# A two-layer graph network on one core: bias by a TensorE product, the row factor folded into the edge weights, and a later sort of the early tiles

## The chip, the cores and the metric

The kernel runs on one core of a Trainium2 chip. The engines that matter here are TensorE (PE), VectorE (DVE), ScalarE (ACT), GpSimd (POOL) and SyncE (SP), which only issues DMAs. Each has its own queue of instructions and works through it in order; they meet at semaphores. The metric is the device time of one execution in microseconds (us), as a median over runs.

## The reference, cut to what matters

N is 4096 nodes, D is 512 features. Every row of `adj` has its diagonal and some eight other entries above zero, all below one.

```python
a = adj + eye(N)
d = sum(a, axis=1) ** (-0.5)
out = (d[:, None] * a * d[None, :]) @ x @ W.T + b     # layer 0
x = layernorm(x + relu(out))
# layer 1: scores masked by max(adj, eye) with 1e16, so that with entries
# below one each node attends to itself alone
x = layernorm(x + x @ wv @ wo)
```

With y = d · (x Wᵀ), row t of layer 0 is d_t · Σ_k w_k · y[col_k] + (d_t · a_tt + d_t) · y_t + b. The first sum goes over the entries off the diagonal.

## The kernel before, in words

Only `few_edges_below_one` runs in the profile; `general` stands behind a test of the data. The 4096 rows are 32 tiles of 128 rows. `adj` is dense in memory (2 MB a tile), and the kernel looks for the few entries itself.

**First pass** (the loop over t in range(NT + 1)). SP loads every tile of `adj` (L545). POOL loads x (L550), PE transposes it (L673) and multiplies it by Wᵀ (L687), ACT copies between (L678), scales the product by d and so makes y (L720), and POOL writes y to memory (L722). ACT also sums the rows of a tile (L694) or, for a tile that DVE scans in this pass, looks for negative entries (L699). `scaling` makes d on POOL (L706, L709).

DVE finds the entries. A tile's *scan* is 16 steps: for each of eight segments of 512 columns one MAX8 (L749) and one FIND_INDEX8 (L750). Its *sort* is some 25 small operations (L753 to L811) over 64 candidates a row. It leaves in `rec` the columns, the weights w and their splits into bf16 pieces. The operations of a sort stand between the steps of the next tile's scan, in the generator `steps`. Then a tile is *matched*: `match` runs six stages (KEY to END, L825 to L876) that permute the rows by their number of edges with small bf16 products on PE (L858, L861) and end in `cols_all` (L872), the columns to be gathered, KH = 9 slots a row.

`EARLY` = 12 tiles are scanned in the first pass as they come, then the five last ones, which stay resident, then the 15 of `again`, which are loaded a second time. `order` is that order, and place n means the n-th tile of it. `RATE` = 7 steps of `steps` are emitted per iteration of the first pass; the rest is spread over the tiles of the second.

**Second pass** (the loop over i in range(NT + 2)). For place i POOL issues nine indirect DMAs (L1077), each of which gathers 128 rows of y; they run up to 18 ahead of PE. ACT builds nine 128 × 128 matrices s_t from the weights (L973 to L986). PE adds up nine products g · s_t (L1280; two records each in the profile). DVE does L1139 (yo ← yo · own + b, with the bias in `b_bc`), L1146 (h ← acc · d + yo) and L1154 (h ← max(h, 0) + x, with its row sum). PE transposes h (L673), ACT copies it (L678), PE multiplies by the product of the two weights of layer 1 (L687), and ACT scales and writes out (L1185). L1173 and L1176 make the variance on DVE. For the last two places DVE sums gathered rows first (`presum`, L1096), and PE's products are at L1104.

SP's queue in the second pass holds, for each place, the load of `yo` (y of the tile itself; three buffers, so it waits for an L1146 three places back) and that of x (which waits for an L1154), and between them the reloads of `adj` (five buffers, which wait for DVE and ACT to be done with an older tile). A reload is issued in the code where `steps` comes to a tile that isn't there.

Of the kernel before, what the change touches and what calls it, by code (L numbers as in the profile page):

```python
# [9 lines left out]
FP = mybir.dt.float32  # L10
# [4 lines left out]
P = 128  # L15
# [404 lines left out]
def few_edges_below_one(  # L420
# [44 lines left out]
    small = ctx.enter_context(tc.tile_pool(name="small", bufs=4))  # L465
    big = ctx.enter_context(tc.tile_pool(name="big", bufs=5))
    wk_ = ctx.enter_context(tc.tile_pool(name="work0", bufs=1))
    recs = ctx.enter_context(tc.tile_pool(name="recs", bufs=8))
    keys = ctx.enter_context(tc.tile_pool(name="keys", bufs=2))
    dram = ctx.enter_context(tc.tile_pool(name="dram", bufs=1, space=bass.MemoryType.DRAM))  # L470
    mt = ctx.enter_context(tc.tile_pool(name="match", bufs=1))
# [78 lines left out]
        engine.dma_start(x_t, x[ts(t, P), :])  # L550
        return x_t

    EARLY, LAG = 12, 5
    last = NT - LAG
    early = [e * last // EARLY for e in range(EARLY)]

# [15 lines left out]
    w_nat, wv = su0[:, 0], su0[:, 1].rearrange("p c d -> p (c d)")  # L572
    nc.scalar.dma_start(w_nat, w0.rearrange("(c p) d -> p c d", p=P))
    wT = p1.tile([P, ND, D], FP, name="wT", bufs=1)
    b_bc = const.tile([P, D], FP, name="b_bc")
    wvo = const.tile([P, ND, D], FP, name="wvo")

    def transpose_w():
        for dc in range(ND):
            pt = ps_t.tile([P, 512], FP, name="pt")  # L580
            for oc in range(ND):
                nc.tensor.transpose(pt[:, ts(oc, P)], w_nat[:, oc, ts(dc, P)], ident)
            nc.scalar.copy(wT[:, dc, :], pt[:, :D])

    def load_second_weights():

# [138 lines left out]

        return rec.bitcast(BF)[:, :, 1::2]

    def extraction(t, a_t, rec):

        v = v_all[:, t, :]
        vu = v.bitcast(U32)
        idx = keys.tile([P, C], U32, name="idx")
        key = keys.tile([P, 2, C], U32, name="key")
        keyf = key.bitcast(FP)
        top = keys.tile([P, 2, K], FP, name="top")
        topu = top.bitcast(U32)
        own = keys.tile([P, E], FP, name="own")  # L740
        mask = keys.tile([P, C], FP, name="mask")
        ints = keys.tile([P, 2, K], U32, name="ints")
        w = rec[:, 1]
        home = slice(t // TS * E, (t // TS + 1) * E)
        long = []
        for s in range(SEGS):
            o = slice(s * E, (s + 1) * E)
            seg = a_t[:, ts(s, SW)]
            long.append(lambda o=o, seg=seg: nc.vector.max(v[:, o], seg))  # L749
            long.append(lambda o=o, seg=seg: nc.vector.max_index(idx[:, o], v[:, o], seg))  # L750

        def stt(out, a, sc, b, op0, op1, **kw):
            return lambda: nc.vector.scalar_tensor_tensor(out, a, sc, b, op0=op0, op1=op1, **kw)  # L753

        def both(a):
            return a.rearrange("p (o c) -> p o c", o=1).to_broadcast([P, 2, a.shape[1]])

        def one(out, a, s1, s2, **kw):
            return lambda: nc.vector.tensor_scalar(out, a, s1, s2, **kw)

        def top8(f, r):
            return lambda: nc.vector.max(top[:, f, r * 8 : r * 8 + 8], keyf[:, f])  # L762

        def drop(f, r):
            return lambda: nc.vector.match_replace(  # L765
                keyf[:, f], top[:, f, r * 8 : r * 8 + 8], keyf[:, f], 0.0
            )

        short = [
            [  # L770

                stt(own, idx[:, home], spot[:, t % TS : t % TS + 1], v[:, home],
                    ALU.is_equal, ALU.mult, accum_out=own_all[:, t : t + 1]),
                stt(key[:, 0], idx, 12, place[:, 0], ALU.logical_shift_left, ALU.bitwise_or),
            ],
            [
                stt(key[:, 1], vu, 0x7FFFF, place[:, 1], ALU.bitwise_and, ALU.bitwise_or),
                stt(key[:, 0], vu, 19, key[:, 0], ALU.logical_shift_right, ALU.bitwise_or),
            ],
            [stt(keyf, both(v), 0.0, keyf, ALU.is_gt, ALU.mult)],  # L780
            [stt(keyf[:, :, home], both(own), 0.0, keyf[:, :, home], ALU.is_equal, ALU.mult)],
            [
                top8(1, 0),
                lambda: nc.scalar.activation(
                    mask, keyf[:, 0], AF.Sign, accum_out=n_all[:, t : t + 1]
                ) if second else nc.vector.tensor_scalar(
                    mask, keyf[:, 0], 0.0, 0.0, op0=ALU.is_gt, op1=ALU.add,
                    accum_out=n_all[:, t : t + 1],
                ),
            ],  # L790
            [drop(1, 0), top8(0, 0)],
            [top8(1, 1), drop(0, 0)],
            [drop(1, 1), top8(0, 1)],
            [top8(1, 2), drop(0, 1)],
            [top8(0, 2)],
            [
                one(ints[:, 1], topu[:, 0], 0xFFF, 19, op0=ALU.bitwise_and,
                    op1=ALU.logical_shift_left),
                one(ints[:, 0], topu[:, 0], 12, 0xFFF, op0=ALU.logical_shift_right,
                    op1=ALU.bitwise_and),  # L800
            ],
            [
                stt(w.bitcast(U32), topu[:, 1], 0x7FFFF, ints[:, 1],
                    ALU.bitwise_and, ALU.bitwise_or),
                lambda: nc.vector.tensor_copy(rec[:, 0], ints[:, 0]),
            ],
            [one(rec[:, 2], w, 0.0, row1n, op0=ALU.is_gt, op1=ALU.mult)],
            [lambda: nc.vector.tensor_tensor(
                rec[:, 3:6], rec[:, 0:3], upper(rec)[:, 0:3], ALU.subtract
            )],  # L810
            [lambda: nc.vector.tensor_tensor(  # L811
                rec[:, 6], rec[:, 4], upper(rec)[:, 4], ALU.subtract
            )],
        ]
        return long, short


    second = []
# [99 lines left out]

    def steps():

        after = [[] for _ in range(STEPS)]
        for n, t in enumerate(order):
            if t not in a_tiles:
                reload()
            edges[t] = dict(rec=recs.tile([P, 7, K], FP, name="rec"))
            long, short = extraction(t, a_tiles[t], edges[t]["rec"])
            begun.append(t)
            for j in range(STEPS):
                long[j]()
                for f in after[j]:  # L930
                    f()
                if j == STEPS - 1:
                    picked.append(t)
                    if t in early:
                        nc.vector.tensor_reduce(
                            deg_all[:, t : t + 1], v_all[:, t, :], AX.X, ALU.add
                        )
                yield
            after = [[] for _ in range(STEPS)]
            for j, fs in enumerate(short):  # L940
                after[j] += fs
            after[len(short)].append(lambda t=t: sorted_.append(t))
        for fs in after:
            for f in fs:
                f()
            yield
# [41 lines left out]

    xs, us = {}, {}
    DEEP = 3  # L990
    RATE = 7
    EARLIER = NT - 7
    due = [(t + 1, t) for t in range(NT) if t not in early]
    for n, t in enumerate(early):
# [15 lines left out]
    for t in range(1, DEEP):  # L1010
        a_tiles[t] = load_first(t)
    transpose_w()
    nc.gpsimd.dma_start(b_bc, bcast_rows(b0, D))
    setup, left = iter(()), None
    for t in range(NT + 1):
        if t == 0:
# [12 lines left out]
            pts.append(transpose_rows(xs.pop(j)))  # L1029
        kind, begin, end = next(setup, (None,) * 3) if len(ahead) < 2 else (None,) * 3  # L1030
        got = begin() if kind == "t" else None
        for j in [j for at, j in due if at == t and j in early]:
            scaling(j)
        if t < NT:
            if t in early:
                sum_negative(t, a_tiles[t])
# [63 lines left out]
    def summed_products(i, pos, c=slice(0, D)):  # L1100

        k = SAME + pos if pos < KH - SAME else None
        g = slots[i * KH if k is None else i * KH + k]
        nc.tensor.matmul(  # L1104
            zs[i][:, c], mats[i][:, KH if k is None else k, :], g[:, c],
            start=(pos == 0), stop=(k is None),
        )

    def build(count):
# [24 lines left out]
        d = d_all[:, t : t + 1]  # L1134
        nc.scalar.activation(own, own, AF.Identity, scale=d, bias=d)  # L1135

    def own_bias(i):
        own = own_all[:, order[i] : order[i] + 1]
        nc.vector.scalar_tensor_tensor(yo[i], yo[i], own, b_bc, op0=ALU.mult, op1=ALU.add)  # L1139

    HALVES = (slice(0, D // 2), slice(D // 2, D))

    def scaled(i, c=slice(0, D)):
        if i not in hs:
            hs[i] = p2.tile([P, D], FP, name="h", bufs=3)
        nc.vector.scalar_tensor_tensor(  # L1146
            hs[i][:, c], zs[i][:, c], d_all[:, order[i] : order[i] + 1], yo[i][:, c],
            op0=ALU.mult, op1=ALU.add,
        )

# [95 lines left out]
    for i in range(NT + 2):  # L1246
        if i < NT:
            zs[i] = ps_a.tile([P, D], FP, name="acc")
        free = len([t for t in scanned if t in picked])
        p = i - 1  # L1250
        has_p = 0 <= p < NT
        for k in range(KH):
# [7 lines left out]
            if i == NT - 1:  # L1260
# [6 lines left out]
                if k == 7:  # L1267
                    pts[i] = transpose_rows(hs[i], (0, 1))
                if k == 8:
                    for n in range(KH - SAME + 1):  # L1270
                        summed_products(i, n, HALVES[1])
                    hTs[i] = p2.tile([P, ND, P], FP, name="hT", bufs=2)
# [6 lines left out]
            elif i < NT:  # L1279
                nc.tensor.matmul(  # L1280
                    zs[i], mats[i][:, k, :], slots.pop(i * KH + k),
                    start=(k == 0), stop=(k == KH - 1),
                )
            if i < NT:
                gather(i * KH + k + AHEAD)
# [26 lines left out]
            t = at("V", i, k)  # L1312
            if t is not None:
                variance(t)
            if k == 6 and i < NT:
                own_bias(i)
            if k == 6 and has_p:
                eps_var(p)
            t = at("F", i, k)
# [45 lines left out]
```

## Time and profile before

| what | value |
|---|---|
| time, median of 3 runs | 649.07 us (648.53 to 650.29) |
| profiled execution, its own time | 647.33 us |
| span of the profile | 645.5 us |
| PE busy | 556.8 us, 86% |
| DVE busy | 543.6 us, 84% |
| ACT busy | 509.1 us, 79% |
| POOL busy | 351.2 us, 54% |
| mean granted PE clock | 0.944 |
| DMA | 222.14 MB, mean 344 GB/s |

A line of the costliest groups names the code line, the engine, the operation, output and inputs and the number of instructions; after the bar stand busy time in us and mean duration in ns, and then the engine's idle time just ahead of them with what ended it. A line of a timeline has its start and duration in us, and in brackets the idle time ahead of it. DVE operations overlap by some 0.08 us, so from start to start they take less than their duration.

### The profile page before, as it was taken

The page shows a single profiled execution, that of the slowest core. Times are in us where ns is not written, and L with a number is a line of the kernel's source. Part 1 is how long each engine was busy: PE and PEld are TensorE (multiplying, and loading weights), DVE is VectorE, ACT ScalarE, POOL GpSimd, SP SyncE. Part 2 cuts the span into 40 slices and gives each one's busy share as a digit, 9 for nine tenths or more (in the row PEclk, how much of TensorE's full clock was granted, in tenths as well). Part 3 has the DMA queues.
Part 4 walks back from the last instruction along what each step waited for, and adds up shares of the span by engine and source line. Part 5 has one row for each costly group of instructions (what it writes and reads, how often), then busy time and mean ns, then how long its engine had stood idle before and what let it go on. Part 6 is the DMA issues. An engine that isn't in the chain of part 4 may idle for free. (4 is left out here: it accounts for less than half of the span.)

```text
span 645.5 us, 7946 instructions
## 1 busy us (share of the span) xinstructions
PE 556.8 (86%) x1604; PEld 258.0 (40%) x1604; DVE 543.6 (84%) x2141; ACT 509.1 (79%) x1121; POOL 351.2 (54%) x464
## 2 busy tenths in 40 slices
PE   1698696888689486999999989999999999999794
PEld 1344342444244132444443434444444444444352
DVE  5679999999999994999999979999999996532431
ACT  1868888779779775999898957999979989994433
POOL 5132421323232377767666757766767777777700
PEclk9599998799879886999999989999999999999798
DMA  8999999999999289999999898999999988888721
GB/s 332 391 427 422 428 421 426 424 421 422 422 428 395 102 263 366 340 411 408 399 401 405 324 391 302 380 382 360 365 404 341 340 268 272 292 270 253 243 70 54
DMA packets 51850, 222.14 MB, mean 344 GB/s; under 512 B 8080, under 2 KB 9104, under 8 KB 45520
## 3 DMA queue, kind: packets, MB, share of 16 engines
q1 hardware_dynamic: 18416, 119.55, 45.6%
q0 software_dynamic: 28240, 92.56, 40.8%
q10 hardware_dynamic: 5136, 9.44, 3.8%
q14 instruction: 43, 0.35, 0.2%
q8 instruction: 15, 0.25, 0.2%
HBM read 204.73 MB, written 16.78 MB: 343 GB/s over the span
## 5 line engine op out<-in xcount | busy, mean ns | idle before, releaser
L1077 POOL DMA_INDIRECT g<-y,cols_all x288 | 281.4, 977 | 112.6 <-issue 41.9
L1280 PE MATMUL acc<-g,s_t 128*128 128x512 f32 x540 | 258.1, 612 | 23.8 <-DMA g<-y,cols_all 13.4
L749 DVE MAX8 v_all<-a_t 128x8 f32<-128x512 f32 x256 | 172.7, 687 | 16.9 <-DMA a_t<-in_adj_dram 16.9
L750 DVE FIND_INDEX8 idx<-v_all,a_t 128x8 uint32<-128x512 f32 x256 | 175.9, 691 | 0.0
L1280 PEld LDWEIGHTS acc<-g,s_t 128*128 128x128 f32 x540 | 98.0, 194 | 140.9 <-issue 92.8
L687 PE MATMUL acc<-wT,xT 128*128 128x512 f32 x256 | 126.6, 647 | 24.1 <-ACT xT L678 24.0
L699 ACT ACTIVATE dump<-a_t 128x2048 uint8<-128x2048 f32 (+1 forms) x52 | 119.5, 2299 | 4.4 <-DMA a_t<-in_adj_dram 4.3
L687 PE MATMUL acc<-wvo,hT 128*128 128x512 f32 x256 | 118.6, 606 | 5.0 <-ACT hT L678 4.6
L687 PEld LDWEIGHTS acc<-wT,xT 128*128 128x128 f32 x256 | 51.1, 207 | 86.9 <-issue 58.1
L687 PEld LDWEIGHTS acc<-wvo,hT 128*128 128x128 f32 x256 | 49.7, 196 | 67.4 <-issue 58.1
L973 ACT ACTIVATE sq<-cols,wr_all 128x128 f32<-128x128 f32 x160 | 58.1, 396 | 0.3 <-ACT hT L678 0.2
L694 ACT ACTIVATE dump<-a_n 128x4096 uint8<-128x4096 f32 x15 | 54.4, 3628 | 4.7 <-DMA a_n<-in_adj_dram 4.6
L977 ACT ACTIVATE s_t<-sq,wr_all 128x128 f32<-128x128 f32 x128 | 57.6, 487 | 0.5
L550 POOL DMA_DIRECT2D x_t<-in_x_dram x32 | 18.0, 562 | 68.1 <-PE pt L673 67.5
L986 ACT ACTIVATE s_t<-s_t,wr_all 128x128 f32<-128x128 f32 x150 | 48.9, 394 | 0.0
L1146 DVE SCALAR_TENSOR_TENSOR h<-acc,d_all,yo 128x512 f32<-128x512 f32 (+1 forms) x33 | 24.0, 727 | 20.9 <-PE acc L1280 15.9
L762 DVE MAX8 top<-key 128x8 f32<-128x64 f32 x192 | 41.0, 221 | 0.5
L678 ACT COPY hT<-pt 128x512 f32<-128x512 f32 x31 | 17.9, 579 | 23.8 <-PE pt L673 22.8
L706 POOL TENSOR_SCALAR deg<-deg_all 128x1 f32<-128x1 f32 x32 | 6.8, 224 | 48.0 <-ACT dump L694 47.9
L1139 DVE SCALAR_TENSOR_TENSOR yo<-yo,own_all,b_bc 128x512 f32<-128x512 f32 x32 | 23.8, 743 | 7.7 <-ACT own_all L1135 7.7
L673 PE MATMUL pt<-ident,x_t 128*128 128x128 f32 x128 | 20.3, 291 | 8.8 <-DVE above L841 7.6
L765 DVE MATCH_REPLACE8 key<-top,key 128x64 f32<-128x64 f32 x128 | 27.2, 214 | 0.0
(128 smaller groups left out, 643.5 us busy)
## 6 DMA issues: line engine op xcount, KB each, us to landing
a_t<-in_adj_dram SPq DMA_DIRECT2D x30, 2048.0 KB, 17.2
a_n<-in_adj_dram SPq DMA_DIRECT2D x15, 2048.0 KB, 17.4
x_t<-in_x_dram POOLq DMA_DIRECT2D x32, 256.0 KB, 11.9
yo<-y SPq DMA_DIRECT2D x32, 256.0 KB, 5.3
x_t<-in_x_dram SPq DMA_DIRECT2D x32, 256.0 KB, 5.6
out_dram<-r_t ACTq DMA_DIRECT2D x32, 256.0 KB, 6.4
g<-y,cols_all POOLq DMA_INDIRECT x288, 7.3
y<-y_t POOLq DMA_DIRECT2D x17, 256.0 KB, 11.9
```

Of the source, the lines that this page charges most:

```text
L687: nc.tensor.matmul(u, srcT[:, dc, :], w[:, dc, :], start=(dc == 0), stop=(dc == ND - 1))
L694: nc.scalar.activation(dump[:, : part.shape[1]], part, AF.Copy, accum_out=dst)
L699: nc.scalar.activation(dump[:, o], a_t[:, o], AF.Relu, scale=-1.0, accum_out=neg_all[:, t, halves[0] : halves[0] + 1],)
L749: long.append(lambda o=o, seg=seg: nc.vector.max(v[:, o], seg))
L750: long.append(lambda o=o, seg=seg: nc.vector.max_index(idx[:, o], v[:, o], seg))
L762: return lambda: nc.vector.max(top[:, f, r * 8 : r * 8 + 8], keyf[:, f])
L765: return lambda: nc.vector.match_replace(keyf[:, f], top[:, f, r * 8 : r * 8 + 8], keyf[:, f], 0.0)
L973: nc.scalar.activation(sq, cols1, AF.Square, bias=wr[:, 2, k : k + 1])
L977: nc.scalar.activation(s_t[:, k, :], away(), AF.Relu, scale=wr[:, 3, k : k + 1], bias=wr[:, 1, k : k + 1],)
L986: nc.scalar.activation(s_t[:, k, :], s_t[:, KH, :], AF.Copy, scale=wr[:, 1, k : k + 1])
L1077: nc.gpsimd.indirect_dma_start(out=slots[j], out_offset=None, in_=y[:, :], in_offset=bass.IndirectOffsetOnAxis(ap=cols_all[:, t, k : k + 1 ...
L1280: nc.tensor.matmul(zs[i], mats[i][:, k, :], slots.pop(i * KH + k), start=(k == 0), stop=(k == KH - 1),)
```

## The change

- The bias leaves DVE. `split_b` writes b as three bf16 pieces into the three rows of `b3`, whose sum is b exactly, with five short DVE operations ahead of the first pass; the broadcast load of `b_bc` goes. In the second pass a product of `ones3` (3 × 128) with `b3` (3 × 512), both bf16, starts each accumulation on PE (`bias`), and the nine products are added to it. `own_bias` goes.
- The row factor d is multiplied into the weights w in the sort (a new DVE operation on 128 × 24), and L1146 becomes h ← yo · own + acc.
- `EARLY` goes from 12 to 14, so 13 tiles are reloaded and not 15; `RATE` goes from 7 to 9.
- `extraction` is divided into `scan` and `sorting`. `sort_some` decides how many waiting tiles are sorted during a scan: none for places 0 and 1, one each for places 2 to 6 (`FULL`), none for 7 to 17, two each from 18 (`HELD`) on. So five tiles are sorted before place 7, and the others in the second pass. The scans' index results wait in 15 `idx` buffers instead of 2; `recs` has 5 buffers instead of 8.
- `scaling` of an early tile is emitted right after the last step of its scan.

```diff
@@ -465,7 +465,7 @@
-    recs = ctx.enter_context(tc.tile_pool(name="recs", bufs=8))
+    recs = ctx.enter_context(tc.tile_pool(name="recs", bufs=5))
     keys = ctx.enter_context(tc.tile_pool(name="keys", bufs=2))
     dram = ctx.enter_context(tc.tile_pool(name="dram", bufs=1, space=bass.MemoryType.DRAM))
     mt = ctx.enter_context(tc.tile_pool(name="match", bufs=1))
@@ -550,7 +550,8 @@
         engine.dma_start(x_t, x[ts(t, P), :])
         return x_t
-    EARLY, LAG = 12, 5
+    EARLY, LAG = 14, 5
+    FULL, HELD = 6, 18
     last = NT - LAG
     early = [e * last // EARLY for e in range(EARLY)]
@@ -572,7 +573,9 @@
     w_nat, wv = su0[:, 0], su0[:, 1].rearrange("p c d -> p (c d)")
     nc.scalar.dma_start(w_nat, w0.rearrange("(c p) d -> p c d", p=P))
     wT = p1.tile([P, ND, D], FP, name="wT", bufs=1)
-    b_bc = const.tile([P, D], FP, name="b_bc")
+    b3 = const.tile([3, D], BF, name="b3")
+    ones3 = const.tile([3, P], BF, name="ones3")
+    nc.gpsimd.memset(ones3, 1.0)
     wvo = const.tile([P, ND, D], FP, name="wvo")
     def transpose_w():
@@ -581,6 +584,19 @@
             for oc in range(ND):
                 nc.tensor.transpose(pt[:, ts(oc, P)], w_nat[:, oc, ts(dc, P)], ident)
             nc.scalar.copy(wT[:, dc, :], pt[:, :D])
+    def split_b():
+        t = [p1.tile([P, D], FP, name="x_t", bufs=6)[:3] for _ in range(3)]
+        nc.gpsimd.dma_start(t[0], bcast_rows(b0, D)[:3])
+        for n in range(2):
+            nc.vector.tensor_tensor(t[n + 1], t[n], t[n].bitcast(BF)[:, 1::2], ALU.subtract)
+        for n in range(3):
+            u, e = t[n].bitcast(BF)[:, 1::2], ident[:3, n : n + 1]
+            if n == 0:
+                nc.vector.tensor_scalar(b3, u, e, None, op0=ALU.mult)
+            else:
+                nc.vector.scalar_tensor_tensor(b3, u, e, b3, op0=ALU.mult, op1=ALU.add)
     def load_second_weights():
@@ -725,14 +741,25 @@
         return rec.bitcast(BF)[:, :, 1::2]
-    def extraction(t, a_t, rec):
+    def scan(t, a_t):
+        v = v_all[:, t, :]
+        idx = keys.tile([P, C], U32, name="idx", bufs=HELD - FULL + 3)
+        long = []
+        for s in range(SEGS):
+            o = slice(s * E, (s + 1) * E)
+            seg = a_t[:, ts(s, SW)]
+            long.append(lambda o=o, seg=seg: nc.vector.max(v[:, o], seg))
+            long.append(lambda o=o, seg=seg: nc.vector.max_index(idx[:, o], v[:, o], seg))
+        return long, idx
+    def sorting(t, idx, rec):
 
 
         v = v_all[:, t, :]
         vu = v.bitcast(U32)
-        idx = keys.tile([P, C], U32, name="idx")
         key = keys.tile([P, 2, C], U32, name="key")
         keyf = key.bitcast(FP)
         top = keys.tile([P, 2, K], FP, name="top")
@@ -742,12 +769,6 @@
         ints = keys.tile([P, 2, K], U32, name="ints")
         w = rec[:, 1]
         home = slice(t // TS * E, (t // TS + 1) * E)
-        long = []
-        for s in range(SEGS):
-            o = slice(s * E, (s + 1) * E)
-            seg = a_t[:, ts(s, SW)]
-            long.append(lambda o=o, seg=seg: nc.vector.max(v[:, o], seg))
-            long.append(lambda o=o, seg=seg: nc.vector.max_index(idx[:, o], v[:, o], seg))
         def stt(out, a, sc, b, op0, op1, **kw):
             return lambda: nc.vector.scalar_tensor_tensor(out, a, sc, b, op0=op0, op1=op1, **kw)
@@ -804,7 +825,10 @@
                     ALU.bitwise_and, ALU.bitwise_or),
                 lambda: nc.vector.tensor_copy(rec[:, 0], ints[:, 0]),
             ],
-            [one(rec[:, 2], w, 0.0, row1n, op0=ALU.is_gt, op1=ALU.mult)],
+            [
+                one(rec[:, 2], w, 0.0, row1n, op0=ALU.is_gt, op1=ALU.mult),
+                one(w, w, d_all[:, t : t + 1], None, op0=ALU.mult),
+            ],
             [lambda: nc.vector.tensor_tensor(
                 rec[:, 3:6], rec[:, 0:3], upper(rec)[:, 0:3], ALU.subtract
             )],
@@ -812,7 +836,7 @@
                 rec[:, 6], rec[:, 4], upper(rec)[:, 4], ALU.subtract
             )],
         ]
-        return long, short
+        return short
 
     second = []
@@ -918,12 +942,24 @@
     def steps():
-        after = [[] for _ in range(STEPS)]
+        waiting = []
+        def sort_some(count):
+            after = [[] for _ in range(STEPS)]
+            for t, idx in [waiting.pop(0) for _ in range(min(count, len(waiting)))]:
+                edges[t] = dict(rec=recs.tile([P, 7, K], FP, name="rec"))
+                short = sorting(t, idx, edges[t]["rec"])
+                for j, fs in enumerate(short):
+                    after[j] += fs
+                after[len(short)].append(lambda t=t: sorted_.append(t))
+            return after
         for n, t in enumerate(order):
             if t not in a_tiles:
                 reload()
-            edges[t] = dict(rec=recs.tile([P, 7, K], FP, name="rec"))
-            long, short = extraction(t, a_tiles[t], edges[t]["rec"])
+            after = sort_some(0 if n < 2 or FULL < n < HELD else 1 if n <= FULL else 2)
+            long, idx = scan(t, a_tiles[t])
             begun.append(t)
             for j in range(STEPS):
                 long[j]()
@@ -935,12 +971,10 @@
                         nc.vector.tensor_reduce(
                             deg_all[:, t : t + 1], v_all[:, t, :], AX.X, ALU.add
                         )
+                        scaling(t)
                 yield
-            after = [[] for _ in range(STEPS)]
-            for j, fs in enumerate(short):
-                after[j] += fs
-            after[len(short)].append(lambda t=t: sorted_.append(t))
-        for fs in after:
+            waiting.append((t, idx))
+        for fs in sort_some(len(waiting)):
             for f in fs:
                 f()
             yield
@@ -988,7 +1022,7 @@
     xs, us = {}, {}
     DEEP = 3
-    RATE = 7
+    RATE = 9
     EARLIER = NT - 7
     due = [(t + 1, t) for t in range(NT) if t not in early]
     for n, t in enumerate(early):
@@ -1010,7 +1044,7 @@
     for t in range(1, DEEP):
         a_tiles[t] = load_first(t)
     transpose_w()
-    nc.gpsimd.dma_start(b_bc, bcast_rows(b0, D))
+    split_b()
     setup, left = iter(()), None
     for t in range(NT + 1):
         if t == 0:
@@ -1029,8 +1063,6 @@
             pts.append(transpose_rows(xs.pop(j)))
         kind, begin, end = next(setup, (None,) * 3) if len(ahead) < 2 else (None,) * 3
         got = begin() if kind == "t" else None
-        for j in [j for at, j in due if at == t and j in early]:
-            scaling(j)
         if t < NT:
             if t in early:
                 sum_negative(t, a_tiles[t])
@@ -1103,7 +1135,7 @@
         g = slots[i * KH if k is None else i * KH + k]
         nc.tensor.matmul(
             zs[i][:, c], mats[i][:, KH if k is None else k, :], g[:, c],
-            start=(pos == 0), stop=(k is None),
+            start=False, stop=(k is None),
         )
     def build(count):
@@ -1134,9 +1166,9 @@
         d = d_all[:, t : t + 1]
         nc.scalar.activation(own, own, AF.Identity, scale=d, bias=d)
-    def own_bias(i):
-        own = own_all[:, order[i] : order[i] + 1]
-        nc.vector.scalar_tensor_tensor(yo[i], yo[i], own, b_bc, op0=ALU.mult, op1=ALU.add)
+    def bias(i, c=slice(0, D)):
+        nc.tensor.matmul(zs[i][:, c], ones3, b3[:, c], start=True, stop=False)
     HALVES = (slice(0, D // 2), slice(D // 2, D))
@@ -1144,7 +1176,7 @@
         if i not in hs:
             hs[i] = p2.tile([P, D], FP, name="h", bufs=3)
         nc.vector.scalar_tensor_tensor(
-            hs[i][:, c], zs[i][:, c], d_all[:, order[i] : order[i] + 1], yo[i][:, c],
+            hs[i][:, c], yo[i][:, c], own_all[:, order[i] : order[i] + 1], zs[i][:, c],
             op0=ALU.mult, op1=ALU.add,
         )
@@ -1246,6 +1278,7 @@
     for i in range(NT + 2):
         if i < NT:
             zs[i] = ps_a.tile([P, D], FP, name="acc")
+            bias(i, HALVES[0] if i == NT - 1 else slice(0, D))
         free = len([t for t in scanned if t in picked])
         p = i - 1
         has_p = 0 <= p < NT
@@ -1267,6 +1300,7 @@
                 if k == 7:
                     pts[i] = transpose_rows(hs[i], (0, 1))
                 if k == 8:
+                    bias(i, HALVES[1])
                     for n in range(KH - SAME + 1):
                         summed_products(i, n, HALVES[1])
                     hTs[i] = p2.tile([P, ND, P], FP, name="hT", bufs=2)
@@ -1279,7 +1313,7 @@
             elif i < NT:
                 nc.tensor.matmul(
                     zs[i], mats[i][:, k, :], slots.pop(i * KH + k),
-                    start=(k == 0), stop=(k == KH - 1),
+                    start=False, stop=(k == KH - 1),
                 )
             if i < NT:
                 gather(i * KH + k + AHEAD)
@@ -1312,8 +1346,6 @@
             t = at("V", i, k)
             if t is not None:
                 variance(t)
-            if k == 6 and i < NT:
-                own_bias(i)
             if k == 6 and has_p:
                 eps_var(p)
             t = at("F", i, k)
```

## The prediction

> **What bounds the kernel now.** I read first the page's busy tenths in 40 slices of 16.1 us, then the costliest groups, then the timelines of the engines, and last the order in which the changed kernel's instructions stand on each engine. The page's chain of waits names only the last instructions, so the bound has to be built from the timelines.
>
> ```profile
> PE   1698696888689486999999989999999999999794
> DVE  5679999999999994999999979999999996532431
> L1077 POOL DMA_INDIRECT g<-y,cols_all x288 | 281.4, 977 | 112.6 <-issue 41.9
> L749 DVE MAX8 v_all<-a_t 128x8 f32<-128x512 f32 x256 | 172.7, 687 | 16.9 <-DMA a_t<-in_adj_dram 16.9
> L1139 DVE SCALAR_TENSOR_TENSOR yo<-yo,own_all,b_bc 128x512 f32<-128x512 f32 x32 | 23.8, 743 | 7.7 <-ACT own_all L1135 7.7
> ```
>
> DVE is full from about 60 to 540 us: scans (L749, L750), sorts, and in the second pass four large operations a tile. PE is full from about 400 to 595 us. So the first pass and the early second pass go at DVE's pace, the later tiles at PE's. The end is neither:
>
> ```profile
> 592.27 0.64 PE L673 MATMUL pt<-ident,h 128*128 128x128 f32 x4
> 592.75 5.32 PE L1280 MATMUL acc<-g,s_t 128*128 128x512 f32 x12
> 602.64 6.20 PE L687 MATMUL acc<-wvo,hT 128*128 128x512 f32 x8 [4.58 <-ACT hT L678]
> 611.25 0.60 PE L673 MATMUL pt<-ident,h 128*128 128x128 f32 x4
> ```
> ```profile
> 595.11 0.75 DVE L1096 SCALAR_TENSOR_TENSOR g<-g,wr_all 128x512 f32<-128x512 f32 x1 [8.21 <-DMA g<-y,cols_all]
> 596.40 0.75 DVE L1096 SCALAR_TENSOR_TENSOR g<-g,wr_all 128x512 f32<-128x512 f32 x1 [0.54 <-DMA g<-y,cols_all]
> 598.78 1.54 DVE L1096 SCALAR_TENSOR_TENSOR g<-g,wr_all 128x512 f32<-128x512 f32 x2 [1.62 <-DMA g<-y,cols_all]
> ```
>
> Call T(n) the start of PE's transposes of h of place n (L673), and h(n) the start of L1146. T(20) is at 509.26, T(27) at 592.27: seven tiles in 83.0 us, 11.86 each, with no idle. T(28) comes 18.98 later, because the presums of place 30 on DVE wait for gathers, the h behind them is late, and PE waits. Between 500 and 600 us POOL issues 79 gathers back to back at 1.27 us, so the tail is bound by gathers, and these run from where a tile's columns (L872) let them.
>
> **The change part by part.** The sum is made against the profiled execution: span 645.5, own time 647.33 (1.83 around it), and the shown median lies 1.74 above that.
>
> *Start of the second pass.* By the built order, DVE stands 57 scan steps further at h(0) (304 for 247), 7 sorts less (7 for 14) and 4 matches less (5 for 9). By start-to-start intervals a step is 0.635 (0.60 for L749; 0.60 plus 0.07 of value load for L750), a sort 3.05, a first-pass match 1.15: +36.2 − 21.4 − 4.6; with `split_b` (five short operations of about 0.6, the 512-column price) +3 and seven `w *= d` at 0.14 (as the row1n operation of L759 ends) +1, some +14.5 in all. Against it stand DVE's 16.9 us of waits for early tiles: the second early tile is now tile 1, not 2, and I take 7.4 of them as filled (between 0 and 11; the first 5.76 cannot go). h(0): 239.15 + 14.5 − 7.4 = 246.3, from 243 to 254. The first gather goes the other way: ACT's last copy L678 now stands ahead of the two half row sums of 1.9 us that hold the last y back, so it starts near 220 instead of 223.25. The first tiles' columns are there before.
>
> *Reloads.* Two of 15 fall away (4.2 MB). The first one stands on SP's queue behind the yo load, which waits for h(0), and the x load, which waits for residual(0):
>
> ```profile
> 239.91 0.33 SPq L1087 DMA_DIRECT2D yo<-y  x1
> 240.65 0.33 SPq L550 DMA_DIRECT2D x_t<-in_x_dram  x1
> 241.07 0.38 SPq L545 DMA_DIRECT2D a_t<-in_adj_dram  x1
> ```
>
> That is 1.9 us after h(0). In the kernel before DVE still had resident tiles to scan, and the load was hidden. Now the scan of place 19 comes right after h(1). Issue at 248.5 and 10.1 us to landing (that same load's) give 258.6, against about 256.5 where DVE is ready: a stall of 2. With 17.2, the median of all such loads, it is 9.
>
> *Second pass.* From h(1) to h(20) DVE has 208 steps (132.1), 22 sorts at 3.05 + 0.14 (70.2), 19 matches at 0.64 (12.2), 19 times L1146 and L1154 (1.27: 24.3) and 18 variances (3.4): 242.2. The same rows for h(1) to h(23) before give 269.6, with 5.9 of waits 275.5, and 281.0 was measured, so I multiply by 1.02: 247. L1139 is gone from it (0.66 a tile). h(1) near 257 gives h(20) at 504, plus 3 of waits (0 to 6): 507, T(20) at 508.4, 0.9 earlier than before. All scans are then done, two places after which DVE was done before, too, so PE sets the pace.
>
> *Tail.* The bias matmul adds to PE. No row has it; the L858 bf16 matmul of 63 columns is followed 0.04 later, so 512 columns make about 0.33; bounds are 0.04 and 0.86, two f32 records of L1280 at 0.43. I take 0.33. It stands a few records ahead of the place where the first product stood and needs the same free accumulator, so it adds no wait: what is behind it on PE waited there before. T(27): 508.4 + 83.0 + 2.3 = 593.7. What changes is the gathers: in the new order the columns (L872) of place 23 stand just ahead of h(20), 1.5 us by the rows between them, and the gathers before them need 11.3 us a tile (9 × 1.25) where DVE needs 13, so POOL waits there without a backlog and the gathers of place 23 begin near 505.5. In the kernel before they began at 508.79, 2.6 us after an L872 at 506.22. From there they run back to back in both, so every later gather goes 3.3 us earlier, and the presums' wait (8.21 + 0.54 + 1.62, of which PE saw 4.58 and a product of 6.20 for 3.60, its clock dropped) all but closes: the wvo product of 602.64 could start at 599.3, and PE would want it at 602.64 − 4.58 + 1.4 + 0.3 = 599.8, 1.4 being the later T(27). T(28): 593.7 + 12.2 = 605.9, not 611.25. From there 34.25 as before and 1 for the last biases: span 641.1, own time 642.9, as a median 644.7.
>
> *At nothing:* the factor d moved into w is 4.5 us of DVE (in the sums above); L1146 with other operands is one operation of the same shape. `scaling` moved to POOL's stream inside the steps costs 0.22 each of an engine 54% busy. Fewer rec buffers could hold a sort back; the order shows at most four alive.
>
> Two rules of the Trainium skill bear on it, and none of the numbers above needs them. "TensorE: Matmul & The Clock Gate", section "Back-to-back issue gap", counts in its formula only the columns moved: about 216 ns for 512, whatever the rows of weights. It speaks against a free bias: 32 of them would be 6.9 us of PE by it (estimate), some 2.2 in the ten last tiles, where my figure gives 3.3.
>
> The gathers that overlap L1139 last 1.01 us, those over L1154 1.08, others 0.954. "GPSIMD Engine Reference", section "1. Specifications", says that GpSimd shares its SBUF interface with VectorE instructions of two SBUF inputs. Rows and rule would give POOL back at most 32 × 0.06 = 1.8 us; the sum takes none of it.
>
> **The rivals.** *Slower: the late reload and DVE behind it.* The reload takes 17.2 us, DVE stalls 9 in place of 2, and has 6 of waits in place of 3: h(20) at 517, T(20) at 518.5, and as PE has no slack afterwards T(28) is at 616 and the span 651.3; median 655 (651 to 662, the top with h(0) at 254). It decides from h(20) later than 511, where the end equals that of before. For it: DMA share is 0.98 from 240 to 400 us, and later reloads landed after 12.0, 13.3 and 13.7. Against: two reloads less, and the first itself landed after 10.1.
>
> *No change, about 650.* Either the gathers do not come earlier, T(28) stays near 611.6 and the span is 646.8 (own 648.6, median 650.4); or the bias costs 0.86, ten times 0.53 more: 650.0. For it: POOL is back to back at the end and has only the early columns to gain from. Against: POOL's stalls for columns in the last tiles are visible (1.53 us ahead of the gather at 602.67).
>
> *The removed L1139 does more than I count:* DVE gains its waits back and the tail closes by h(18): below 640.
>
> **How the numbers follow.** The forecast, 640 to 647, has 0.51; below 640 0.05; no change 0.16; slower 0.28. A run of this kernel tells about 0.3% from nothing, that is 647.1 to 651.0. Faster 0.56, same 0.16, slower 0.28. The forecast's own range is 639 to 647; since both signs hold weight, the whole range goes from 637 to 658: some 0.1 of the slower case lies above, 0.03 below. The predicted time is 644.5.
>
> **What would show it.** First gather near 220; h(0) near 246; the first reload issued about 2 us after h(0), and DVE's wait ahead of the first scan of a reloaded tile 0 to 3 us; h(20) near 507; the bias matmul followed 0.2 to 0.4 us later by the next record; T(27) to T(28) 12 us instead of 19, last gather near 609. The prediction is wrong if DVE still scans after h(21), or if T(28) stays at 611 with T(20) early: then gathers, not columns, are the tail's limit.

## The result, and the profile after

The change makes the kernel slower: 655.41 us median of 7 runs (653.9 to 658.08) against 650.99 (648.53 to 652.28) for the kernel before, a ratio of 1.0074 with a 95% interval of 1.0049 to 1.0099. The profiled execution took 653.9, its span is 652.1. The prediction had 644.5.

The page of the changed kernel, busy tenths in 40 slices of 16.3 us:

```profile
PE   1699877487979485899999999999999999999993
DVE  5799999999999994989999999999999544312521
```

DVE is full until about 510 us and then nearly free; before, it was full until 540. So DVE did get its work back. The groups that answer to those shown of before (L1139 is gone, L1171 is new):

```profile
L1109 POOL DMA_INDIRECT g<-y,cols_all x288 | 280.2, 973 | 116.9 <-issue 46.6
L752 DVE MAX8 v_all<-a_t 128x8 f32<-128x512 f32 x256 | 165.7, 676 | 9.7 <-DMA a_t<-in_adj_dram 9.7
L1171 PE MATMUL acc<-b,ones 3*128 3x512 bf16 x31 | 11.6, 384 | 0.0
```

The scans wait 9.7 us for adj in place of 16.9, and PE has 11.6 us of new records. PE is now full from 280 us to the end, and the hole (a stretch in which it waits) that the kernel before had near 600 us is gone. Two windows of each kernel show what PE gets done meanwhile; the columns are the window, its length, the busy time of PE and of PEld (the weight loads) with the number of records, the granted clock, the DMA share and GB/s. Only the nine products are counted (18 records a place). The kernel before:

```profile
220.00:400.00 180.00, 117.16 (x233) 42.41 (x234) 0.93 0.95 358
220.00:580.00 360.00, 241.25 (x504) 91.43 (x504) 0.97 0.95 347
```

The changed kernel:

```profile
220.00:400.00 180.00, 115.09 (x230) 40.91 (x230) 0.94 0.95 353
220.00:580.00 360.00, 233.77 (x486) 87.03 (x486) 0.97 0.93 332
```

At 400 us the changed kernel is 3 records behind, a sixth of a place. At 580 us it is 18 behind, a whole place or some 12 us. The records alone overstate how much of that is lost after 400 us, since in the changed kernel the transposes and wvo products stand further back among them: T(10) comes 5.91 later than before (398.09 for 392.18), T(20) 8.79 and T(27) 12.25. In the 180 us from 400 to 580 PE was busy for 178.58 before and 179.24 after: it has next to no slack in either, and more to do for each place. PE's timeline around place 28:

```profile
592.20 0.66 PE L689 MATMUL pt<-ident,h 128*128 128x128 f32 x4
...
604.52 0.66 PE L689 MATMUL pt<-ident,h 128*128 128x128 f32 x4
605.01 5.32 PE L1314 MATMUL acc<-g,s_t 128*128 128x512 f32 x12
610.16 3.60 PE L703 MATMUL acc<-wvo,hT 128*128 128x512 f32 x8
613.60 2.74 PE L1314 MATMUL acc<-g,s_t 128*128 128x512 f32 x6
616.27 0.38 PE L1171 MATMUL acc<-b,ones 3*128 3x512 bf16 x1
616.58 0.66 PE L689 MATMUL pt<-ident,h 128*128 128x128 f32 x4
```

T(27) is at 604.52 and T(28) at 616.58, 12.06 apart where it had been 18.98. DVE's waits between 560 and 625 us (total, times, longest) have 0.3 us in all for the presums' gathers, where the kernel before waited 8.21 + 0.54 + 1.62; what L1128 waits for is ACT's first part of the sum:

```profile
DVE sums L1205 <- ACT dump L1194: 18.7, 3, 7.0
DVE g L1128 <- ACT g L1126: 14.1, 2, 7.7
...
DVE g L1128 <- DMA g<-y,cols_all: 0.3, 1, 0.3
```

The wait that PE saw did close, but T(27) itself is 12.25 later than before, so of the 12.25 only 6.9 come back, and with 1.3 more behind T(28) (35.52 for 34.25, the last biases) the span ends 6.6 later.

### The profile page after: what moved, and what is told of

Read it like the earlier page. It is cut to its first block, busy times and chain, and to the rows that moved or that the text cites. A ratio compares the mean times of both kernels' runs of the same rounds, so it can differ in the third digit from the quotient of the medians.

```text
span 652.1 us, 7998 instructions
## 1 busy us (share of the span) xinstructions
PE 565.1 (87%) x1637; PEld 258.1 (40%) x1637; DVE 527.5 (81%) x2114; ACT 504.2 (77%) x1143; POOL 350.7 (54%) x465
## 5 line engine op out<-in xcount | busy, mean ns | idle before, releaser
L752 DVE MAX8 v_all<-a_t 128x8 f32<-128x512 f32 x256 | 165.7, 676 | 9.7 <-DMA a_t<-in_adj_dram 9.7
L753 DVE FIND_INDEX8 idx<-v_all,a_t 128x8 uint32<-128x512 f32 x256 | 172.9, 683 | 0.2 <-issue 0.2
L703 PE MATMUL acc<-wvo,hT 128*128 128x512 f32 x256 | 115.4, 593 | 0.6 <-ACT hT L1334 0.6
L710 ACT ACTIVATE dump<-a_n 128x4096 uint8<-128x4096 f32 x13 | 47.3, 3637 | 0.0
L1205 DVE TENSOR_SCALAR sums<-sums 128x1 f32<-128x1 f32 x32 | 6.5, 202 | 43.2 <-ACT dump L1194 43.2
L1178 DVE SCALAR_TENSOR_TENSOR h<-yo,own_all,acc 128x512 f32<-128x512 f32 (+1 forms) x33 | 23.9, 723 | 19.3 <-PE acc L1314 12.8
L783 DVE MAX8 top<-key 128x8 f32<-128x64 f32 x192 | 36.1, 214 | 0.4
L1194 ACT ACTIVATE dump<-acc 128x512 f32<-128x512 f32 x32 | 18.6, 583 | 14.9 <-PE acc L703 12.8
L694 ACT COPY xT<-pt 128x512 f32<-128x512 f32 x32 | 18.4, 596 | 10.5 <-PE pt L689 10.5
## 6 DMA issues: line engine op xcount, KB each, us to landing
y<-y_t POOLq DMA_DIRECT2D x18, 256.0 KB, 11.6
```

Of the source, the lines that this page charges most:

```text
L694: copy = nc.scalar.copy(dst.rearrange("p c s -> p (c s)"), pt[:, :D])
L703: nc.tensor.matmul(u, srcT[:, dc, :], w[:, dc, :], start=(dc == 0), stop=(dc == ND - 1))
L710: nc.scalar.activation(dump[:, : part.shape[1]], part, AF.Copy, accum_out=dst)
```

## The experiments

All times are medians; the kernel before ran beside each group at 650.12, 650.60, 650.39 and 650.35. Four theories are named in the expectations. P: PE bounds the second pass, and the bias product is what slows it. D: DVE, the deferred sorts and the late reload bound it. T: the tail's gathers set the end. S: the split of b costs by its place in the first pass. The first gather, quoted for several runs, is the first instruction of the second pass on POOL: the later it comes, the later the second pass begins.

| run | us | ratio to before, 95% interval |
|---|---|---|
| nobias | 647.86 | 0.9967 [0.9945, 0.9989] |
| dve_all | 646.48 | 0.9960 [0.9929, 0.9991] |
| dve_late | 651.84 | 1.0027 [1.0001, 1.0054] |
| b_bias_pe | 659.24 | 1.0150 [1.0100, 1.0201] |
| nosplit | 650.11 | 1.0000 [0.9979, 1.0022] |
| split_pool | 654.96 | 1.0077 [1.0048, 1.0107] |
| bias_behind | 655.99 | 1.0088 [1.0060, 1.0116] |
| sched_only | 646.29 | 0.9944 [0.9913, 0.9975] |
| twice | 657.84 | 1.0116 [1.0073, 1.0159] |
| defer_off | 679.25 | 1.0441 [1.0408, 1.0473] |
| early12 | 668.76 | 1.0263 [1.0221, 1.0306] |
| split_first | 651.38 | 1.0023 [0.9997, 1.0049] |

### Is it the bias on PE?

nobias takes the product out and nothing else:

```diff
-        nc.tensor.matmul(zs[i][:, c], ones3, b3[:, c], start=True, stop=False)
+        return
-                    start=False, stop=(k == KH - 1),
+                    start=(k == 0), stop=(k == KH - 1),
```

> The changed kernel with the bias left out altogether (the three-row product is not issued, the first of the nine products starts the accumulation); the output lacks b. Theory P: PE is the bound from about 400 us on, and each bias product takes some 0.5 us of it (places 15 to 27 go at 12.4 us each, 11.9 before); 18 to 20 places lie behind 400 us, so the time falls by 9 to 11, from 655.4 to 644 to 647, and if the wait for gathers at place 28 comes back in part, to 650. Rival D: the deferred sorts and the late reload set the time, the bias costs nothing: 654 to 656, as with it.

647.86, 7.5 below the changed kernel: theory P, a little short of its 9 to 11. Rival D falls. Why it is short shows in PE's waits from 280 to 520 us (total, times, longest). With the product:

```profile
PE acc L1314 <- DMA g<-y,cols_all: 1.5, 4, 0.5
PE pt L856 <- ACT rank_key L849: 0.8, 1, 0.8
```

Without it:

```profile
PE acc L1314 <- DMA g<-y,cols_all: 7.0, 8, 2.1
PE pt L856 <- ACT rank_key L849: 2.4, 4, 0.8
```

Without the product PE waits 7.1 us more there, so up to T(20) most of the 20 products' price falls into waits, and T(20) gains only 2.5 (515.53 for 518.05).

What a bias costs PE is read from the timelines. The changed kernel at place 20:

```profile
517.53 0.27 PE L856 MATMUL pt<-ident,rank_key 128*128 128x128 f32 x1
517.74 0.38 PE L1171 MATMUL acc<-b,ones 3*128 3x512 bf16 x1
518.05 0.66 PE L689 MATMUL pt<-ident,h 128*128 128x128 f32 x4
518.55 3.60 PE L1314 MATMUL acc<-g,s_t 128*128 128x512 f32 x8
```

Without the bias, at place 19 (at place 20 PE waits 0.62 us for ACT there; in the changed kernel place 19 takes the same 1.02 us, 505.13 to 506.15, as place 20):

```profile
502.66 0.27 PE L856 MATMUL pt<-ident,rank_key 128*128 128x128 f32 x1
502.76 0.60 PE L689 MATMUL pt<-ident,h 128*128 128x128 f32 x4
503.20 3.60 PE L1314 MATMUL acc<-g,s_t 128*128 128x512 f32 x8
```

From the match transpose to the first product it is 1.02 us with the bias and 0.54 without: 0.48 a place. Of these 0.31 pass from the bias's start to the next one's; 0.11 is the longer gap ahead of it (0.21 for 0.10), and 0.06 the longer stretch of the transposes behind it (0.50 for 0.44).

dve_all gives the bias back to DVE and drops the product, the split and `b3`; the factor d stays in the weights:

```diff
+        nc.vector.scalar_tensor_tensor(yo[i], yo[i], own, b_bc, op0=ALU.mult, op1=ALU.add)
...
+            nc.vector.scalar_tensor_tensor(
+                hs[i][:, c], zs[i][:, c], 1.0, yo[i][:, c], op0=ALU.mult, op1=ALU.add
+            )
```

> The changed kernel with the bias on DVE again for all places (one operation a place, about 0.66 us from start to start, and the three-row product goes), everything else of the change kept: the factor d in the weights, 14 early tiles, the later sorts. Theory P: PE gets 0.5 us a place back where it is the bound, DVE loses 0.66 a place where it is close to the bound (places 2 to 20): 648 to 655. Rival D: DVE is the bound up to place 20 and all of 20 times 0.66 comes on top: 664 to 669.

646.48, a little better than P had it and 18 away from D. DVE took 32 more operations of 0.66 and the kernel became 9 faster. Part of the 9 is the split, which this kernel drops too (below); against the kernel that keeps the product and leaves the split out (nosplit, 650.11) it is 3.6, with intervals that just overlap. So although DVE is full up to some 500 us, the bias seems to cost more on PE than on DVE.

dve_late puts the bias on DVE from place 12 on (`by_dve(i)` is i >= 12; one index buffer less and the mask `kept` in bf16 make room for `b_bc`):

> The changed kernel with the bias on PE for places 0 to 11 and on DVE for places 12 to 31. Theory P: PE gets 0.5 us back for 15 to 20 places, DVE has slack by then since it ends its scans at 511 us: 645 to 649. Rival D: DVE, full up to 511 us, ends its scans 9 times 0.66 later and the end moves with it: 658 to 662. Theory T, that the tail's gathers set the end: no change, 654 to 656.

651.84, 3.6 below the changed kernel, but not the 645 to 649 of P. Two things were left out of that expectation: the split is still in this kernel (see below), and PE, with less to do, meets a wait in the tail again (4.60 us at 601.04 for DVE's permutation).

b_bias_pe is the other corner: the kernel before with the bias by PE, which brings the split of b with it, and d in the weights (for which d is computed right after a scan).

> The kernel before with only the bias by PE and the factor d in the weights (12 early tiles, 7 steps an iteration, every tile sorted in the scan after it; d of an early tile is computed right after its scan, which the new factor needs). Theory P: PE, the bound from about 400 us on, gets 0.5 us a place more: 10 us, of which the idle of 7 us at place 28 may take up to 7: 654 to 661 against 651. Rival D: the bias product costs nothing and DVE gets 21 us back: 640 to 648.

659.24, inside P's range; bias and split together, without the new schedule, make the kernel before 9 slower. D, which had it faster, is out. Its first gather came at 229.37 (223.25 before), so not all of the 9 is the product's, though the expectation counted the product alone.

### What the split of b costs

dve_all's first gather came at 220.64, the changed kernel's at 224.79. DVE's timeline of the changed kernel, where the split stands between the steps of its first scans (these steps are left out at the dots):

```profile
20.31 0.69 DVE L752 MAX8 v_all<-a_t 128x8 f32<-128x512 f32 x1 [1.21 <-DMA a_t<-in_adj_dram]
23.90 0.47 DVE L597 TENSOR_SCALAR b<-x_t,ident 3x512 bf16<-3x512 bf16 x1 [2.90 <-DMA x_t<-in_L_gnn_b_dram]
...
24.97 0.66 DVE L593 TENSOR_TENSOR x_t<-x_t 3x512 f32<-3x512 f32 x1
...
26.17 0.66 DVE L593 TENSOR_TENSOR x_t<-x_t 3x512 f32<-3x512 f32 x1
26.76 0.73 DVE L599 SCALAR_TENSOR_TENSOR b<-x_t,ident,b 3x512 bf16<-3x512 bf16 x1
...
28.09 0.72 DVE L599 SCALAR_TENSOR_TENSOR b<-x_t,ident,b 3x512 bf16<-3x512 bf16 x1
```

DVE works in order, so a scan whose data is there waits behind L597 for b: 2.90 of wait and 3.1 of work. From 60 us to the second pass DVE has no hole to make it good. nosplit sets `b3` to zero on POOL in place of the split:

> The changed kernel with the bias products kept and the split of b left out (POOL sets b3 to zero instead; the output lacks b). Theory S: in the changed kernel DVE waits 2.9 us at 21 us for b's load and needs 3.1 more for the five operations; DVE is full from there to the second pass, so the last loads (189.4 us; 185.3 where the bias was on DVE and nothing was split) and the first gather (224.8; 220.6) come 4 us late: without the split the first gather is near 220.6 and the time 4 to 5 lower, 650 to 652. Rival: the start of the second pass is set by ACT and the loads alone: first gather at 224 to 225, time 654 to 656.

650.11, first gather at 220.04. Theory S holds: in this run the scan that began at 20.31 goes on without a wait. The 6 us at 21 us come out as 5 at the end.

split_pool moves the five operations to POOL in the fifth iteration (seven there, with the sums apart), with the load where it was:

> The changed kernel with b loaded at the same place, but split on POOL in the fifth iteration of the first pass, so that DVE neither waits for the load nor works on it. Theory S: as without the split, 650 to 652. Rival: 654 to 656; or POOL, which also starts loads of x and computes d, passes its delay on: above 655.

654.96: nothing gained. POOL stood 5.96 us for b and 2.84 for buffers and was done only at 43.2 us; the loads of x that stand behind it on its queue came late, and DVE waited 4.1 us for a match on PE instead. The cost had moved, as the second half of the rival says.

split_first has b's load first on SP's queue and the split first in DVE's order (in the trace the two subtractions run ahead of the first scan, the three writes of b3 between its steps):

```diff
+        nc.sync.dma_start(t[0], bcast_rows(b0, D)[:3])
...
+    split_b()
     a_tiles = {0: load_first(0, 4)}
```

> The changed kernel with b's load put first on SP's queue and the five operations of the split first in DVE's order, where DVE has nothing to do until the first part of adj lands at 5.8 us. Theory S (the split costs by its place: DVE stood 2.9 us for b's load and 3.1 us for the work in the full stretch): the first scan starts at 6 to 7, the first gather at 220 to 222, time 650 to 652, as with the split left out. If the cost is in the buffers that the split takes from the loads of x, not in DVE's time: 654 to 656.

651.38, first gather at 221.55. The first scan started at 8.22 and not at 6 to 7, since adj landed later too, but the 4 us are back. So it was the place in DVE's order and of the load on its queue, not the buffers taken.

### Can the bias product be had cheaper on PE?

bias_behind emits it behind the transposes and ahead of the first product:

> The changed kernel with the bias product emitted behind the transposes of h of the place two back and right ahead of the first of the nine products, not ahead of the transposes. From start to start the bias takes 0.31 us, but a place takes 0.46 to 0.53 more than without it. If the rest is the break between the small matmuls around it (match transpose, bias, transpose of h), its new place saves up to 0.2 a place: 651 to 653. If the price is the product's own, no change: 654 to 656.

655.99, no change. The transposes then take 0.53 to the bias (0.44 without) and the bias 0.32, so a place takes 0.42 more than without it in place of 0.48: the break in the stream goes with the product.

twice issues it twice:

> The changed kernel with the bias product issued twice for each place (the output has 2b). Theory P: a second product of the same shape right behind the first takes 0.31 us of PE, as the row from the first to its successor does; 20 of the 32 stand where PE has no idle: 6 to 8 more than 655.4, 661 to 664. Rivals D and T (DVE, or the tail's gathers, set the time): 654 to 656.

657.84, 2.4 more: the direction of P, the size too small. In its timeline the second product starts 0.23 behind the first, so the second in a row is cheaper than the lone one, and 20 of them make 4.6; the intervals of the two kernels (ratios 1.0049 to 1.0099 and 1.0073 to 1.0159) don't tell 2.4 from that, nor from nothing.

### What the schedule is worth

sched_only is the change without bias, split and factor: 14 early tiles, 9 steps, the late sorts, d right after the scan.

> Only the schedule of the change: 14 early tiles, 9 steps an iteration, the later sorts and d computed right after a scan; bias and row factor on DVE as in the kernel before (no three-row product, no split, no d in the weights). With the factor d in the weights this took 646.5 (0.996 of before). Theory P: DVE has room, so 4.5 us less of DVE work changes nothing that shows: 645 to 648, ratio 0.993 to 0.998. Rival: DVE still bounds the early second pass: 642 to 644.

646.29, ratio 0.9913 to 0.9975 of before: this beats both kernels. Its first gather, in POOL's timeline:

```profile
218.92 1.06 POOL L1093 DMA_INDIRECT g<-y,cols_all  x1 [2.59 <-DMA y<-wo]
```

That is 4.3 earlier than the 223.25 before, and the time is 4.3 lower. That the two numbers agree is not shown to be cause and effect: T(20) is only 0.65 earlier (508.61 for 509.26), and the rest comes and goes in the tail. Against dve_all (646.48) it has 4.5 us less on DVE, and no difference shows.

defer_off is sched_only with every tile sorted in the scan after it (`sort_some(1)`, 8 `recs`, 2 `idx` buffers):

> The schedule of the change alone, but every tile sorted in the scan after it (14 early tiles, 9 steps an iteration, bias and row factor on DVE as before). If DVE's work ahead of the last loads sets the start of the second pass, the eight sorts that come back into the first pass put 8 x 3.05 = 24 us ahead of them: first gather at 235 to 243 in place of 218.9, time 660 to 670. If ACT and the loads set it: first gather near 220, time 645 to 649.

679.25, first gather at 249.76: further than expected, in the direction of the first reading. With 14 scans ahead of the last loads the sorts must go; DVE's order sets the start.

early12 is sched_only with 12 early tiles and 7 steps; the late sorts stay:

> The schedule of the change alone, but with 12 early tiles and 7 steps an iteration as before, so that only the late sorts are left of it. If DVE's work ahead of the last loads sets the start, two scans (20 us) and some sorts less bring the first gather to 205 to 214, and the time falls to 636 to 644 if PE is the bound from there on. If DVE, which then has two scans and two reloads more behind the start, bounds the second pass: 648 to 656. If ACT's row sums, two more of 3.6 us, set the start: first gather at 219 to 224, 646 to 651.

668.76, worse than any of the three. DVE waited 27.3 us for adj in the first pass (its first gather is at 221.57), and the scans not done there stood before the sorts in the second: PE waited 21.3 us for permutations. The two halves of the schedule only pay together.

## Why the prediction was wrong

**The step that failed** is "h(20) at 504, plus 3 of waits (0 to 6): 507, T(20) at 508.4". The first half was near: DVE reached h(20) at 510.65. The second half put T(20) 1.4 after it. DVE's and PE's timelines of the changed kernel have

```profile
510.65 0.74 DVE L1178 SCALAR_TENSOR_TENSOR h<-yo,own_all,acc 128x512 f32<-128x512 f32 x1
```
```profile
518.05 0.66 PE L689 MATMUL pt<-ident,h 128*128 128x128 f32 x4
```

7.40 apart; and the kernel before had 8.64, on the same lists of h and T that the prediction drew on:

```profile
500.62 0.73 DVE L1146 SCALAR_TENSOR_TENSOR h<-acc,d_all,yo 128x512 f32<-128x512 f32 x1
```
```profile
509.26 0.60 PE L673 MATMUL pt<-ident,h 128*128 128x128 f32 x4
```

T(20) stands in PE's order behind products of place 21 and a wvo product, and PE had no hole to speak of from 400 us on, which the prediction says itself. So an earlier h brings nothing there, and what counts is PE's work per place from 280 us on: not ten biases, but every one that stands where PE has no idle. The span missed the predicted 641.1 by 11.0: 6.0 of it is this lag (7.40 for 1.4), 3.65 is h(20) (510.65 for 507), 1.2 the seven places from T(20) to T(27) (86.47 for 85.3), and what is behind T(27) nearly nothing.

What made T(20) late can be read from three runs, by one profiled execution of each. It is at 508.61 in sched_only, at 513.43 in nosplit, which adds the bias product and d in the weights, and at 518.05 in the changed kernel, which adds the split: 4.8 for the one and 4.6 for the other. That 508.61 lies next to the predicted 508.4 is luck, since h(20) was at 501.52 there.

With the lag of the kernel before and the measured price, 507 + 8.64 + 83.0 + 7 x 0.48 + 12.3 + 35.25 gives a span of 649.6 and a median near 653. The forecast would not have been "faster". (The lag is no constant: it is 7.09 in sched_only and 7.50 in nosplit. It only shows that h was there before PE came to it.)

**The bias** was priced at 0.33 a place, from a row of 63 columns. To the next instruction it is 0.31; in the stream it costs 0.48, for the gap ahead of it and the longer transposes behind. From T(20) to T(27), where PE does not wait, it shows whole (86.47 for 83.01, 0.49 a place). The Trainium skill's "TensorE: Matmul & The Clock Gate", section "Back-to-back issue gap", has some 216 ns for an isolated product of 512 columns. The second of two in a row took 0.23, which agrees; the lone one between f32 products took twice that.

**The split** was in the sum at 3 us, as work. The wait for its load was not, nor that DVE's order would make a scan wait behind it. "The first gather near 220" holds to 0.1 us in the kernel without the split (220.04); in the changed kernel it was 224.79.

**The gathers.** The prediction had place 23's begin at 505.5 and the wait at place 28 close because they came 3.3 earlier. The wait closed, and 12.06 was measured for 12.2, but for another reason: the 208th gather (the first of place 23) was at 511.91 and the 270th at 592.18, both some 3 us later than before (508.79, 588.67), and PE was 12 us later, so they were in time.

**Right:** h(0) at 245.47 (246.3); the reload issued 2.0 us after h(0) at 247.45 (248.5), and DVE's wait for it, 1.49 us (2). SP's and DVE's timelines:

```profile
246.24 0.33 SPq L1119 DMA_DIRECT2D yo<-y  x1
247.06 0.33 SPq L550 DMA_DIRECT2D x_t<-in_x_dram  x1
247.45 0.42 SPq L545 DMA_DIRECT2D a_t<-in_adj_dram  x1
```

```profile
259.46 0.69 DVE L752 MAX8 v_all<-a_t 128x8 f32<-128x512 f32 x1 [1.49 <-DMA a_t<-in_adj_dram]
```

Two slips in the sums change nothing: 36.2 − 21.4 − 4.6 + 3 + 1 is 14.2 and not 14.5, and 19 times 1.27 is 24.1 and not 24.3.

DVE's scans end by h(20), the last at 500.1, and the factor d costs nothing that shows (dve_all, with it, 646.48; sched_only, without, 646.29). POOL's gathers went from 977 to 973 ns on average, 288 x 0.004 = 1.2 us in all, within the 1.8 allowed.

**The rivals.** "Slower" had 655, and 655.41 was measured, but its mechanism did not happen: the reload landed in time. "The bias costs more", under no change, named the right engine, but with a price too high (0.86 for 0.48) and a count too small (ten), and without the split. The ledger by runs is: schedule, 650.6 to 646.3, −4.3; bias from DVE to PE with d in the weights, 646.3 to 650.1 (sched_only to nosplit), +3.8; split, 650.1 to 655.4, +5.3. Each of these differences has an uncertainty of some 2 to 2.5 us by the intervals of the two ratios it is taken from.

The parts add up within that: bias and split on the old schedule cost 9.1 (b_bias_pe, 659.24 for 650.12), which is 3.8 + 5.3, and with the schedule's −4.3 it makes the 4.8 between 650.6 and 655.4. That they agree to the tenth is luck. The 3.8 is a difference of two prices: without any bias, but with the split, the kernel took 647.86, 7.5 less than with the product (15 or 16 places of 0.48), so DVE's operation costs some 3.7 where it is (worked out from these runs, not measured by itself; with their intervals it may be anything from near nothing to 7).

## What to carry to other kernels

Where two engines are both full, moving work from one to the other must be priced on the one that receives it, place by place, and not from the slack the giver gets; the test is which engine's queue the end follows back through. Before the lag between two engines' events is assumed, it is read from the trace for the same pair. A short setup step on an engine that works in order costs its place in the queue and the landing of its load, not only its work.

## What the runs showed of the hardware

A lone bf16 product of 512 columns in a stream of f32 products cost 0.48 us (0.42 right ahead of the first product, in bias_behind), though its successor started 0.31 behind it, and a second one in a row only 0.23. After a hole of 3.44 us PE came back slower, in sched_only's timeline:

```profile
589.09 2.74 PE L1305 MATMUL acc<-g,s_t 128*128 128x512 f32 x6
595.26 0.24 PE L866 MATMUL pt<-rec,perm 128*128 128x63 bf16 x1 [3.44 <-DVE perm L857]
595.31 0.29 PE L869 MATMUL pt<-rec,perm 128*128 128x28 bf16 x4
595.44 1.09 PE L674 MATMUL pt<-ident,h 128*128 128x128 f32 x4
596.33 7.50 PE L1305 MATMUL acc<-g,s_t 128*128 128x512 f32 x12
```

Twelve records took 7.50 us there and 5.32 in the stream (605.01 in the changed kernel), and the transposes 1.09 for 0.66: a hole of 3.4 us cost some 2.6 more. The granted clock was 0.68 from 595 to 604 us, and 1.00 in the changed kernel from 604 to 610. The price does not follow the hole's length: in dve_late a hole of 4.60 us cost 1.7 (6.67 and 1.02, clock 0.77 from 601 to 608.5).
